# A graph-attention kernel: gathers of steps 2 and 3 held one by one, picks begun at the seventh group and three lots shorter

## The chip, the cores and the metric

The kernel runs on one core of a Trainium2 chip. The metric is the time of one execution in microseconds of the device. The kernel before has a median of 1760.69 us in 3 runs (1760.31 to 1761.43).

## What is computed

One layer of a graph network with attention over edges, followed by a residual addition and a layer norm. There are 6,250 nodes and 206,250 edges, sorted by destination, with 64 channels in 4 heads of 16.

```python
Qh = (x @ Wq.T + bq).reshape(n, H, D)
Kh = (x @ Wk.T + bk).reshape(n, H, D)
Vh = (x @ Wv.T + bv).reshape(n, H, D)
Ee = (edge_attr @ We.T + be).reshape(-1, H, D)
score = (Kh[src] * Qh[dst] * (1.0 / np.sqrt(D)) * Ee).sum(-1)
score = jnp.exp(jnp.clip(score, -5.0, 5.0))
msg = Vh[src] * score[..., None]
wV = jax.ops.segment_sum(msg, dst, num_segments=n)
x = layernorm(x + wV.reshape(n, H * D))
```

The rows of k and v at the source of every edge (`Kh[src]`, `Vh[src]`) are at random places. How they are brought to the edges is what the change is about.

## The kernel before, in words

**Tiles, groups and steps.** A tile is 128 edges, one a partition. Eight tiles are a group `g`; there are 202 groups (0 to 201, the last with four tiles). Two groups are a step, up to group 193; the last eight groups are steps of their own. A step's k and v (`kv`, 256 numbers of a row for each edge, 16 tiles) live in one of five buffers `kvs`, which are used in turn.

**The prologue.** PE multiplies all nodes by the weights (`ps`, L453), and the products go through SBUF to tables in DRAM: `kv_tab` (k and v of each node, float32) and `q3_tab`. Meanwhile POOL gathers (`collect`, L340) the x rows of the sources of the first five groups, 40 tiles, each gather being held by one of PE's matmuls. For these groups k and v are computed on the spot: ten times `x_turned` (PE, ACT), a matmul, and an addition of the bias on DVE (`first_kv`, L538), numbered i = 0 to 9. From group 5 on k and v are gathered from `kv_tab`. The gathers of groups 5, 6 and 7 (the rest of step 2, and step 3) are issued in that loop over i, behind the additions.

**Gathers.** `gather_kv` (L251) is an indirect DMA on POOL's queue: it brings 128 rows of `kv_tab`, one tile. `lots(s)` lists a step's tiles as two lots a group, and `alone` splits lots to single tiles. `gather` issues the DMAs of a lot in order, and makes the first one of the lot wait for a given instruction (`behind`), so that POOL's queue keeps a chosen place beside the other engines.

**Picks.** The last two tiles of some groups are not gathered. They are computed by PE from the node features in SBUF: for four such tiles together (a lot of picks, two groups, 512 edges) DVE makes one-hot matrices of the sources (`hots`, L640, up to five units in one instruction), and PE multiplies them with the node features, which are kept as three bf16 parts (`picks`, recorded at L680, the line of the helper `product`: 25 units of two blocks of 128 nodes, three matmuls each, 75 matmuls 128x512 a lot, accumulated in one of two PSUM banks `pick`). Then `picked` (DVE) chooses the half, `picked_kv` (PE) multiplies by the weights of k and v, and `place_kv` (ACT) puts the four tiles where the gathers would have put them. `first_unit(g)` tells at which unit iteration g starts: a lot of picks is spread over three iterations, with 9, 8 and 8 units. `when(k)` is its inverse. `LAST` is the number of lots (65). Lot m is ready in iteration `READY[m]`, and the groups it serves are `READY[m] + 4` and `READY[m] + 5`: groups (6, 7), (9, 10), (12, 13), and so on, up to (198, 199).

**The main loop.** Iteration g works on group g, and ahead of it: it issues the loads of edge features (`et`, three steps ahead), query windows (`qw`, four groups ahead) and keys (`kb`, six groups ahead) on SP's queue, and the gathers of the step four steps ahead on POOL's. On DVE: `prod` (k times the turned query-edge product `qe`), the score, one half of the hot tiles of iteration g + 1, the message `qe`, the other half, two subtractions that split the message into three bf16 parts (between them ACT makes the copies `msg`), the one-hot matrix `of` of a step (in odd iterations), the addition of a step's sums to the accumulator, and `term` for group g + 2. On PE, in this order: the edge product `ee` of group g + 3, the second half of a ready lot (`picked_kv`), the picks of iteration g, the transposes `qe` of group g + 1, the queries `qq` of group g + 2, and the sums of a step (`room`, 16 matmuls, every other iteration). On ACT: the exponential, the two halves of `to`, the two `msg` copies, `eb`.

The order of all this is written out by hand: instructions stand on each engine in the order of the source. The gathers of iteration g are held by the last matmul at several marks within the iteration (`where`). Two lines hold the picks' timetable:

```python
return UNITS * (g // 3) + (0, 9, 17)[g % 3]
LAST = max(m for m in range(1, NG) if when(UNITS * m - 1) + 5 < NG)
```

The last groups have no picks: the last lot is finished in iteration 194, and iterations 195 to 201 run without. After the last group come its sums, a layer norm of the last two blocks and their stores; the other blocks are normed and stored within the loop.

Of the kernel before, what the change touches and what calls it, by code (L numbers as in the profile page):

```python
# [22 lines left out]
NG = -(-T // G)  # L23
# [26 lines left out]
def tiles_of(g):  # L50
    return min(G, T - g * G)
# [6 lines left out]
def groups_of(s):  # L58
    return range(STEPS[s][0], STEPS[s][0] + STEPS[s][1])
# [4 lines left out]
BATCH = 4  # L64
UNITS = NB // 2
MOST = 5
XG = 5


def first_unit(g):  # L70

    return UNITS * (g // 3) + (0, 9, 17)[g % 3]


def when(k):

    return max(g for g in range(3 * k // UNITS + 3) if first_unit(g) <= k)


LAST = max(m for m in range(1, NG) if when(UNITS * m - 1) + 5 < NG)  # L80
BEGIN = [when(UNITS * m) for m in range(LAST)]
READY = [when(UNITS * m + UNITS - 1) for m in range(LAST)]
PICKED = [(READY[m] + 4, READY[m] + 5) for m in range(LAST)]
ALL_PICKED = {g for pair in PICKED for g in pair}
assert len(ALL_PICKED) == 2 * LAST and min(ALL_PICKED) > XG
assert all(BEGIN[m + 1] > BEGIN[m] + 1 for m in range(LAST - 1))

# [7 lines left out]
def is_picked(g, j):  # L95

    return g in ALL_PICKED and j >= tiles_of(g) - 2
# [23 lines left out]
def tile_gnn(ctx: ExitStack, tc: tile.TileContext, x, by_rows, xT, wT, bias, beT, weT, eT, src, src_rows, dst,  # L121
# [89 lines left out]
    def fetch_sources(m, pool):  # L211

        if m < LAST:
            SRC[m] = pool.tile([P, BATCH * P], I32, name="srcs")
            nc.sync.dma_start(SRC[m], src_rows[m:m + 1, :].to_broadcast([P, BATCH * P]))

    def sources(m, from_, odd):
        if m < LAST:
            FROM[m], ODD[m] = from_, odd
            nc.scalar.activation(FROM[m], SRC[m], AF.Identity, bias=from_row, scale=0.5)  # L220
            nc.vector.tensor_scalar(ODD[m], SRC.pop(m), 1, None, op0=OP.bitwise_and)
# [8 lines left out]
    def onehot_rows(g, to):  # L230

        n = tiles_of(g)
        TO[g] = to
        nc.scalar.activation(TO[g][:, :n, :],  # L234
                             KB.pop(g)[:, :n * P].rearrange("p (j e) -> p j e", j=n),
                             AF.Square, bias=minus_row3[:3 * W])

    def onehot_rows_rest(g):
        n = tiles_of(g)
        nc.scalar.activation(TO[g][:, :n, :], TO[g][:, :n, :], AF.Relu, bias=one_p[:3 * W],  # L240
                             scale=-1.0)

    def keys(t0):

        n = min(KEYS, T - t0)
        nc.vector.tensor_scalar(key_i[:, :n], dst_i[:, t0:t0 + n], P - 1, None, op0=OP.bitwise_and)
        nc.vector.tensor_copy(key[:, t0:t0 + n], key_i[:, :n, None].to_broadcast([P, n, 2]))
# [7 lines left out]
    def lots(s):  # L255

        some = []
        for g in groups_of(s):
            js = [j for j in range(tiles_of(g)) if not is_picked(g, j)]
            some += [(g, js[:len(js) // 2]), (g, js[len(js) // 2:])]  # L260
        return some

    def alone(some):

        return [(g, [j]) for g, js in some for j in js]
# [6 lines left out]
    def gather(lot):  # L272
        (g, js), after = lot
        for j in js:
            ins = gather_kv(g, j)
            if j == js[0]:
                behind(ins, after)

    with tc.tile_pool(name="nodes", bufs=1) as nodes, \
# [14 lines left out]
        x_nodes = slots[1][:, :30 * C], slots[3][:, :20 * C]  # L294
        src_x = nodes.tile([P, XG * G], I32, name="src_x")
        nc.scalar.dma_start(src_x, src[:, :XG * G])
        w_sb = nodes.tile([C + 1, 3 * C], F32, name="w_sb")
# [35 lines left out]
        x_rows = kvs[KVB - 1].rearrange("p t (u c) -> p (t u) c", u=2)  # L333
        XS = [x_rows[:, g * G:(g + 1) * G, :] for g in range(XG - 1)]
        XS.append(nodes.tile([P, G, C], F32, name="xs"))
        first_tiles = [(g, j) for g in range(XG) for j in range(G)]
        mark = []

        def collect(g, j):
            ins = nc.gpsimd.indirect_dma_start(  # L340
                out=XS[g][:, j, :], out_offset=None, in_=x[:, :],
                in_offset=bass.IndirectOffsetOnAxis(ap=src_x[:, g * G + j:g * G + j + 1], axis=0))
            if mark:
                behind(ins, mark[-1])
# [100 lines left out]
        for i in range(NB // CB):  # L445
            bs = slice(i * CB, (i + 1) * CB)
            kv_sb = chunks.tile([P, CB, 2 * C], F32, name="kv_sb")
            for b in range(0, CB, 2):
# [38 lines left out]
                pair = (i * CB + b) // 2  # L487
                for _ in range(1 + (pair >= NB // 2 - (XG - 1) * G + NB // 2)):
                    collect(*first_tiles.pop(0))
# [34 lines left out]
        def x_turned(g, h):  # L524
            tp = npsum.tile([P, 2, P], F32, name="tp", bufs=2)
            for u in range(2):
                j = 4 * h + 2 * u
                nc.tensor.transpose(tp[:, u, :], XS[g][:, j:j + 2, :].rearrange("p j c -> p (j c)"),
                                    ident)
            xe = nodes.tile([P, 2, P], F32, name="xe", bufs=2)  # L530
            nc.scalar.activation(xe, tp, AF.Copy)
            return xe

        def first_kv(g, h, xe):
            pv = npsum.tile([P, 4, 2 * C], F32, name="pv", bufs=2)
            for u in range(2):
                nc.tensor.matmul(pv[:, 2 * u:2 * u + 2, :], xe[:, u, :], wkv, start=True, stop=True)
            return nc.vector.tensor_add(kv_of(g)[:, 4 * h:4 * h + 4, :], pv,  # L538
                                        bkv_all[:, None, :].to_broadcast([P, 4, 2 * C]))

        def parts_of_x(i, part):

            us = slice(i * 5, (i + 1) * 5)
            xu = x_nodes[i // 3].rearrange("p (u t c) -> p u t c", t=2, c=C)[:, i % 3 * 5:][:, :5]
            if part == 2:
                nc.vector.tensor_sub(parts[:, us, 2], xu, parts[:, us, 1])
            else:
                nc.scalar.activation(parts[:, us, part], xu, AF.Copy)
                if part == 0:
                    nc.vector.tensor_sub(xu, xu, parts[:, us, 0])  # L550

        order = [(g, h) for g in range(XG) for h in range(2)]
        to_gather = lots(2)[2:] + lots(3)
        xe = x_turned(*order[0])
        for k in range(3):
            parts_of_x(k, 0)
        for i, gh in enumerate(order):
            following = x_turned(*order[i + 1]) if i + 1 < len(order) else None
            added = first_kv(*gh, xe)
            xe = following  # L560
            if i < 3:
                parts_of_x(i, 1)
                parts_of_x(i, 2)
            if i in (3, 4):
                parts_of_x(i, 0)
                parts_of_x(i, 1)
                parts_of_x(i, 2)
            if i in (1, 2, 4, 5, 6, 7):
                gather((to_gather.pop(0), added))
            if i == 5:  # L570
                sources(0, early_from, early_odd)
                keys(0)
            if i > 4 and i - 5 < 4:
                onehot_rows(i - 5, early_to[i - 5])
                onehot_rows_rest(i - 5)
# [17 lines left out]
    with tc.If(rv == 0) as branch:  # L593

        with tc.tile_pool(name="work", bufs=2) as work, \
# [32 lines left out]
            def pieces(g):  # L628

                some, k, end = [], max(first_unit(g), 0), min(first_unit(g + 1), UNITS * LAST)  # L630
                while k < end:
                    some.append((k, min(end, k + MOST, (k // UNITS + 1) * UNITS)))
                    k = some[-1][1]
                return some

            def hots(k, end):
                m, lo, hi = k // UNITS, k % UNITS, (end - 1) % UNITS + 1
                HOT[k] = work.tile([P, MOST, BATCH * P], BF16, name="hot", bufs=5)
                shape = [P, hi - lo, BATCH * P // 2, 2]
# [501 lines left out]
```

## Time and profile before

| what | value |
|---|---|
| median of 3 runs | 1760.69 us |
| the profiled execution | 1760.28 us |
| its span, first to last instruction | 1758.4 us |
| TensorE clock granted, mean | 0.990 |
| prod of group 0 starts at | 80.00 us |
| prod of group 201 starts at | 1747.27 us |
| gathers of k and v on POOL | 1312 |

A row of a timeline shows the start in us, the duration in us, the engine, the line, the operation, output and inputs, and in brackets the idle time of the engine before it, with what ended it. A row of the windows shows a stretch, its length, the busy time and number of instructions of PE, PEld (PE's weight loads), DVE, ACT and POOL, the granted clock, the share of the DMA engines' time and GB/s. A row of the groups shows line, engine, operation, names and count, then the busy time in us, the mean of one in ns, the idle time of the engine before them, and what ended most of it. In the chain rows stand the start, the duration and what the chain ran through.

### The profile page before, as it was taken

To read this page: it belongs to the slowest core of one execution; us is meant where nothing else is said; L and a number is where in the kernel's file an instruction comes from. 1 tells how busy PE (TensorE), PEld (TensorE's weight loads), DVE (VectorE), ACT (ScalarE), POOL (GpSimd) and SP (SyncE) were. 2 spreads that over 40 slices of the span, in tenths; PEclk is the share of its full clock that TensorE was granted. 3 is DMA by queue.
4 is the path that set the end of the run, shared out by engine and by line. 5 is a ranking of instruction groups with operands and counts; after the bars stand their busy time and mean duration, and the time that the engine had idled before them with its cause. 6 is when DMAs were issued, how large, how long until landed. Compare 5 with 4: busy or idle time off the path is not lost.

```text
span 1758.4 us, 27231 instructions
## 1 busy us (share of the span) xinstructions
PE 1697.8 (97%) x8717; PEld 900.2 (51%) x8863; DVE 1599.2 (91%) x2711; ACT 924.7 (53%) x1516; POOL 1303.4 (74%) x1362
## 2 busy tenths in 40 slices
PE   6799999999999999999999999999999999999994
PEld 6445555555555555455555555555555555555543
DVE  5699999999999999999999999999999999999987
ACT  3655555555555555555555545545555555555553
POOL 6777777777777777777777777777777777777752
PEclk9999999999999999999999999999999999999996
DMA  6844444434444445444444444444544434445431
GB/s 190 273 131 120 140 120 127 138 110 139 139 113 140 124 122 141 119 140 129 124 139 116 131 139 111 136 138 118 144 119 135 138 110 138 138 116 144 120 95 29
DMA packets 141939, 229.89 MB, mean 131 GB/s; under 512 B 70369, under 2 KB 71115, under 8 KB 141673
## 3 DMA queue, kind: packets, MB, share of 16 engines
q1 hardware_dynamic: 98086, 139.63, 26.6%
q0 software_dynamic: 43264, 87.38, 19.2%
q8 instruction: 71, 1.16, 0.3%
q10 hardware_dynamic: 436, 1.04, 0.3%
q14 instruction: 82, 0.67, 0.1%
HBM read 220.11 MB, written 7.81 MB: 130 GB/s over the span
## 4 chain that ended last, share of the span: by engine, by line
PE 77%; DVE 12%; DMA 5%; ACT 2%; issue 2%; POOL 1%; SPq 0%; DVEq 0%; ACTq 0%; POOLq 0%
PE pick L680 54%; PE ee L680 10%; PE room L680 6%; PE qe L709 4%; DMA kv<-kv_tab,src_i 4%; DVE hot L640 3%; PE qq L680 3%; DVE score L731 1%; DVE prod L728 1%; DVE term L704 1%; PE ps L453 1%; DVE qe L749 1%; ACT msg L761 1%; DVE qe L766 1%; POOL kv L251 1%
## 5 line engine op out<-in xcount | busy, mean ns | idle before, releaser
L251 POOL DMA_INDIRECT kv<-kv_tab,src_i x1312 | 1263.6, 963 | 411.2 <-issue 162.2
L680 PE MATMUL pick<-hot,parts 128*128 128x512 bf16 x4729 | 1073.7, 379 | 7.7
L680 PEld LDWEIGHTS <-parts 128*128 128x128 bf16 x4875 | 477.2, 98 | 604.6 <-issue 74.7
L640 DVE TENSOR_TENSOR hot<-from,still 128x2560 bf16<-128x2560 bf16 (+2 forms) x384 | 482.4, 1256 | 0.0
L737 ACT ACTIVATE score<-score 128x32 f32<-128x32 f32 x202 | 46.3, 229 | 624.8 <-DVE score L733 620.5
L761 ACT ACTIVATE msg<-qe 128x512 bf16<-128x512 f32 x400 | 238.8, 597 | 154.0 <-DVE qe L749 132.7
L680 PE MATMUL ee<-et,we_sb 128*128 128x512 f32 x404 | 223.4, 635 | 5.5 <-ACT eb L691 4.1
L240 ACT ACTIVATE to<-to,one_p 126x1024 bf16<-126x1024 bf16 x198 | 226.4, 1144 | 0.0
L234 ACT ACTIVATE to<-kb,minus_row 126x1024 bf16<-126x1024 bf16 x198 | 223.8, 1130 | 0.0
L766 DVE TENSOR_TENSOR msg<-qe,msg 128x512 bf16<-128x512 f32 x200 | 136.9, 685 | 70.8 <-ACT msg L761 70.7
L680 PE MATMUL room<-msg,of 128*128 128x192 bf16 x1592 | 150.9, 248 | 16.8 <-DVE acc L803 16.8
L704 DVE TENSOR_TENSOR term<-eb,qq 128x512 f32<-128x512 f32 x202 | 136.7, 677 | 20.6 <-PE qq L680 15.7
L680 PEld LDWEIGHTS <-of 128*128 128x128 bf16 x1600 | 128.9, 99 | 40.5 <-issue 36.6
L731 DVE TENSOR_REDUCE score<-prod 128x32 f32<-128x512 f32 x202 | 138.3, 685 | 7.0
L766 DVE TENSOR_TENSOR qe<-qe,msg 128x512 f32<-128x512 f32 x200 | 138.0, 690 | 4.8 <-ACT msg L761 4.8
L691 ACT ACTIVATE eb<-ee,be_col 128x512 f32<-128x512 f32 x202 | 139.7, 692 | 4.7 <-PE ee L680 4.7
L728 DVE TENSOR_TENSOR prod<-kv,qe 128x512 f32<-128x512 f32 x202 | 137.2, 679 | 5.0 <-issue 2.1
L749 DVE TENSOR_TENSOR qe<-kv,score 128x512 f32<-128x512 f32 x200 | 138.9, 695 | 1.8 <-ACT score L737 1.8
L709 PE MATMUL qe<-ident,term 128*128 128x128 f32 x806 | 122.7, 275 | 1.0 <-DVE term L704 0.9
L720 DVE TENSOR_TENSOR of<-still,key 128x2048 bf16<-128x2048 bf16 (+2 forms) x105 | 122.6, 1168 | 0.2
L709 PEld LDWEIGHTS qe<-ident,term 128*128 128x128 f32 x806 | 101.5, 142 | 41.7 <-DVE term L704 1.9
L680 PE MATMUL qq<-to,qw 126*64 126x512 bf16 x396 | 80.7, 404 | 0.0
(136 smaller groups left out, 875.1 us busy)
## 6 DMA issues: line engine op xcount, KB each, us to landing
et<-in_eT SPq DMA_DIRECT2D x100, 512.0 KB
kb<-key_tab SPq DMA_DIRECT2D x201, 252.0 KB
kv<-kv_tab,src_i POOLq DMA_INDIRECT x1312
srcs<-in_src_rows SPq DMA_DIRECT2D x65, 256.0 KB
qw<-q_tab SPq DMA_DIRECT2D x202, 15.8 KB
kv_tab<-kv_sb SPq DMA_DIRECT2D x4, 640.0 KB
q_tab<-q SPq DMA_DIRECT2D x5, 480.0 KB
acc<-in_x SPq DMA_DIRECT2D x48, 32.0 KB
```

The lines of the kernel that those rows point to most:

```text
L234: nc.scalar.activation(TO[g][:, :n, :], KB.pop(g)[:, :n * P].rearrange("p (j e) -> p j e", j=n), AF.Square, bias=minus_row3[:3 * W])
L240: nc.scalar.activation(TO[g][:, :n, :], TO[g][:, :n, :], AF.Relu, bias=one_p[:3 * W], scale=-1.0)
L251: return nc.gpsimd.indirect_dma_start(out=kv_of(g)[:, j, :], out_offset=None, in_=kv_tab[:, :], in_offset=bass.IndirectOffsetOnAxis(ap=src ...
L640: nc.vector.tensor_tensor(HOT[k][:, :hi - lo].rearrange("p b (a c) -> p b a c", c=2), pairs(FROM[m])[:, None].to_broadcast(shape), block2[ ...
L680: mark.append(nc.tensor.matmul(*aps, **kw))
L704: nc.vector.tensor_mul(TERM[g][:, :n], EB.pop(g)[:, :n], qq[:, :n])
L709: nc.tensor.transpose(qe[g % 2][:, 2 * u:2 * u + 2, :].rearrange("p j c -> p (j c)"), TERM[g][:, u, :], ident)
L728: nc.vector.tensor_mul(prod[:, :n, :], kv_of(g)[:, :n, :C], qe[g % 2][:, :n, :])
L731: nc.vector.tensor_reduce(score, prod[:, :n, :].rearrange("p g (h d) -> p g h d", h=H), axis=AX.X, op=OP.add)
L749: nc.vector.tensor_mul(to.rearrange("p g (h d) -> p g h d", h=H), kv_of(g)[:, :n, C:].rearrange("p g (h d) -> p g h d", h=H), SCORE[g][:, ...
L761: nc.scalar.activation(part, left, AF.Copy)
L766: nc.vector.tensor_sub(left if i == 0 else part_of(g, 2)[1], left, part)
```

## The change

Three things are changed, and all else stays.

- The picks begin in iteration 6 (`LEAD`) and not in iteration 0. Lot m keeps its three iterations and its distance to the groups it serves, so the first lot now serves groups 12 and 13. Groups 6, 7, 9 and 10 are gathered whole.
- `LAST` is computed with 8 in place of 5. There are 62 lots, the last of which is finished in iteration 191 and serves groups 195 and 196. Groups 198 and 199 are gathered whole. With the four tiles of each lot that is gone, 1,324 tiles are gathered in place of 1,312.
- In the prologue the gathers of groups 5, 6 and 7 are 24 in place of 20. They are single tiles (`alone`), each held by the addition of k and v after which it is issued: two after each of the additions 0 to 4, three after each of 5 to 8, two after 9. Before, lots of four and three were issued after the additions 1, 2, 4, 5, 6 and 7, and only the first of a lot was held.

```diff
+LEAD = 6
 XG = 5
 def first_unit(g):
-    return UNITS * (g // 3) + (0, 9, 17)[g % 3]
+    return UNITS * ((g - LEAD) // 3) + (0, 9, 17)[(g - LEAD) % 3]
 def when(k):
-    return max(g for g in range(3 * k // UNITS + 3) if first_unit(g) <= k)
+    return max(g for g in range(LEAD + 3 * k // UNITS + 3) if first_unit(g) <= k)
-LAST = max(m for m in range(1, NG) if when(UNITS * m - 1) + 5 < NG)
+LAST = max(m for m in range(1, NG) if when(UNITS * m - 1) + 8 < NG)
...
-        to_gather = lots(2)[2:] + lots(3)
+        to_gather = alone(lots(2)[2:] + lots(3))
...
-            if i in (1, 2, 4, 5, 6, 7):
+            for _ in range(3 if 4 < i < 9 else 2):
                 gather((to_gather.pop(0), added))
```

Lines after the new one stand one lower in the changed kernel: L251 becomes L252.

## The prediction

> **What bounds the kernel now.** First the page: how full each engine is, and the chain that ended last.
>
> ```profile
> span 1758.4 us, 27231 instructions
> PE 1697.8 (97%) x8717; PEld 900.2 (51%) x8863; DVE 1599.2 (91%) x2711; ACT 924.7 (53%) x1516; POOL 1303.4 (74%) x1362
> PE 77%; DVE 12%; DMA 5%; ACT 2%; issue 2%; POOL 1%; SPq 0%; DVEq 0%; ACTq 0%; POOLq 0%
> ```
>
> PE looks like the bound and POOL like an idle engine. The groups and a window of six iterations in mid-run (the last row counts POOL's gathers up to 1679.7 us) say more:
>
> ```profile
> L251 POOL DMA_INDIRECT kv<-kv_tab,src_i x1312 | 1263.6, 963 | 411.2 <-issue 162.2
> L728 DVE TENSOR_TENSOR prod<-kv,qe 128x512 f32<-128x512 f32 x202 | 137.2, 679 | 5.0 <-issue 2.1
> ...
> 329.90:380.00 50.10, 49.89 (x263) 25.91 (x265) 46.60 (x77) 26.18 (x42) 38.00 (x40) 1.00 0.45 125
> ...
> L251 POOL DMA_INDIRECT kv<-kv_tab,src_i x1280 | 1233.2, 963 | 390.5 <-issue 156.7 <-PE pick L680 95.4 <-DMA kv<-kv_tab,src_i 60.4
> ```
>
> In 50.10 us PE is busy 49.89 at clock 1.00: the loop runs at PE's pace, 8.35 us an iteration. But POOL is just as full in another sense. Its 1,280 gathers up to 1679.7 us take 963 ns plus 390.5/1280 = 305 ns of "idle" each, and 0.30 us is the gap that stands before a gather even when nothing is waited for (rows below). So POOL issues without a pause, one gather in (1233.2 + 390.5)/1280 = 1.268 us. The prod row says that this hurts nobody: in 202 iterations the first reader of the gathered rows was kept idle 5.0 us. What remains is how far POOL is ahead:
>
> ```profile
> 56.21 0.95 POOL L251 DMA_INDIRECT kv<-kv_tab,src_i  x1 [0.30 <-DVE parts L546]
> ...
> 1569.69 0.94 POOL L251 DMA_INDIRECT kv<-kv_tab,src_i  x1 [0.30 <-PE pick L680]
> ...
> 1678.50 1.07 POOL L251 DMA_INDIRECT kv<-kv_tab,src_i  x1 [0.30 <-PE pick L680]
> 1682.54 0.94 POOL L251 DMA_INDIRECT kv<-kv_tab,src_i  x1 [2.96 <-PE qq L680]
> 1699.87 0.94 POOL L251 DMA_INDIRECT kv<-kv_tab,src_i  x1 [7.65 <-PE qq L680]
> 1708.30 0.94 POOL L251 DMA_INDIRECT kv<-kv_tab,src_i  x1 [1.25 <-PE room L680]
> 1729.71 0.94 POOL L251 DMA_INDIRECT kv<-kv_tab,src_i  x1 [0.30 <-PE room L680]
> ```
>
> Counting gathers by group, 1569.69 is the last of group 183 and 1678.50 that of group 196. Only for groups 197, 198 and 199 is POOL held by PE (2.96, 7.65 and 1.25 us, less 0.30 each: 10.96 in all). The last gather starts at 1729.71, 28.7 us before the end.
>
> **The change part by part.** *Counts.* Sixty-five lots of picks (25 units of three matmuls) become 62, and iterations 0 to 5 and 192 to 201 have none; before, only 195 to 201. Gone are 225 pick matmuls on PE, 18 hot tiles on DVE, three srcs loads on SP's queue. Added are 12 gathers on POOL: four in groups 6 and 7, four in 9 and 10, four in 198 and 199. Inside 6 to 191 every lot keeps its place by threes and by even and odd groups, so the loop keeps its pace.
>
> *The stretch that goes.* DVE's timeline gives the iterations by their prod (iterations 177, 186, 194, 195 and 201 here):
>
> ```profile
> 1555.93 0.68 DVE L728 TENSOR_TENSOR prod<-kv,qe 128x512 f32<-128x512 f32 x1
> ...
> 1634.70 0.69 DVE L728 TENSOR_TENSOR prod<-kv,qe 128x512 f32<-128x512 f32 x1
> ...
> 1701.09 0.69 DVE L728 TENSOR_TENSOR prod<-kv,qe 128x512 f32<-128x512 f32 x1 [0.19 <-issue]
> 1704.53 0.70 DVE L766 TENSOR_TENSOR qe<-qe,msg 128x512 f32<-128x512 f32 x1 [0.82 <-ACT msg L761]
> 1706.06 0.69 DVE L766 TENSOR_TENSOR msg<-qe,msg 128x512 bf16<-128x512 f32 x1 [0.23 <-ACT msg L761]
> 1707.26 0.68 DVE L728 TENSOR_TENSOR prod<-kv,qe 128x512 f32<-128x512 f32 x1
> ...
> 1747.27 0.41 DVE L728 TENSOR_TENSOR prod<-kv,qe 128x256 f32<-128x256 f32 x1
> ```
>
> The new kernel has 186 iterations with picks, like iterations 0 to 185 of the old one; the other nine, 1707.26 - 1634.70 = 72.56 us, go, and nine without picks come. Such an iteration is shown by 1701.09 to 1707.26: 6.17 us, not PE's but the chain prod, score, exp, msg on ACT, subtraction, msg, term, in which DVE waits for ACT.
>
> *The front* (DVE's timeline again).
>
> ```profile
> 76.86 0.69 DVE L704 TENSOR_TENSOR term<-eb,qq 128x512 f32<-128x512 f32 x1 [1.68 <-ACT eb L691]
> 77.47 2.61 DVE L640 TENSOR_TENSOR hot<-y,still 128x2560 bf16<-128x2560 bf16 x2
> 80.00 0.68 DVE L728 TENSOR_TENSOR prod<-kv,qe 128x512 f32<-128x512 f32 x1
> ...
> 92.15 1.21 DVE L720 TENSOR_TENSOR of<-still,key 128x2048 bf16<-128x2048 bf16 x1
> ...
> 109.53 0.35 DVE L797 TENSOR_REDUCE room<-room 128x64 f32<-128x192 f32 x1
> ...
> 110.11 0.68 DVE L704 TENSOR_TENSOR term<-eb,qq 128x512 f32<-128x512 f32 x1
> ...
> 118.68 0.68 DVE L728 TENSOR_TENSOR prod<-kv,qe 128x512 f32<-128x512 f32 x1
> ...
> 127.04 0.68 DVE L728 TENSOR_TENSOR prod<-kv,qe 128x512 f32<-128x512 f32 x1
> ```
>
> The two hot tiles at 77.47 go, so prod 0 starts 2.53 us sooner. Iterations 0, 2 and 4 take 6.17. Odd ones also make `of` (about 1.14 to the next start), of which 0.92 hides in the wait for ACT (1704.53 + 0.61 to 1706.06): 6.39, and with the add of iteration 3 (109.53 to 110.11, 0.58) 6.97. Iteration 5 already makes the hot tiles of iteration 6 and takes what it takes now, 127.04 - 118.68 = 8.36. Sum: 3 x 6.17 + 6.39 + 6.97 + 8.36 = 40.23, less 2.53: 37.70. From there PE must do at once what it had not to do in old iteration 0, the sums of a step (the chain in order of time):
>
> ```profile
> 80.18 5.56 PE pick L680 x25
> ...
> 100.70 1.43 PE room L680 x16
> ```
>
> so +1.43. (The pick row prices what left: 225 x 5.56/25 = 50 us of PE, only partly replaced by shorter work, since the nine iterations are now DVE's and ACT's.)
>
> *PE's clock.* An idle PE is a new state for the front. The windows of the tail show one (the third number from the end is the clock).
>
> ```profile
> 1720.00:1740.00 20.00, 10.10 (x43) 6.10 (x40) 16.97 (x40) 8.63 (x16) 8.21 (x9) 0.69 0.17 43
> 1740.00:1760.00 20.00, 8.81 (x42) 7.72 (x42) 10.76 (x35) 5.01 (x9) 0.00 (x0) 0.50 0.03 8
> ```
>
> With PE half busy the granted clock fell to 0.69 and 0.50, so the first picks of iteration 6 may run at half speed. Bounds: nothing (the window at 329.90, clock 1.00) to a whole iteration's 5.56 us of picks done twice as slowly; I take 1.7, nearer the lower end, because work comes back without a gap. The Trainium skill, "TensorE: Matmul & The Clock Gate", Part 1, speaks against the change here: the array falls to half its clock after an idle window of some 3.4 us and needs as long a busy one to come back. By that rule an estimate of the loss is half of 3.4, about 1.7 us; the falling clock in the two rows agrees with it.
>
> *The tail.* Iterations 192, 193 and 194 cost 6.17, 6.39 + 0.78 for a full add, 6.17: 19.5. Their x pick and copies replace the same in 195 and 196. Loop alone: 1758.4 - 72.56 + 37.70 + 1.43 + 1.7 + 19.5 = 1746.2.
>
> *The gathers.* Eight more by group 196 and no pause: the gather at 1678.50 moves to 1688.6 (8 x 1.268). Its holds vanish, because PE's marks come 12 us sooner and POOL 10 us later. From there 36 gathers instead of 32, at 1.249 (the spacing in the last rows, 0.94 + 0.30) to 1.268: the last starts at 1733.6 to 1734.3. Landing:
>
> ```profile
> 1704.86 2.38 DMA kv<-kv_tab,src_i
> ```
>
> 2.38 us from start: 1736.0 to 1736.7, where prod 201 can begin; now it is followed by 1758.4 - 1747.27 = 11.1 us. End by the gathers: 1747.1 to 1747.8. The loop alone would bring prod 201 at 1735.1, so **POOL sets the end, at 1747.5**. Waiting for k and v one by one costs nothing: POOL reaches the prologue's gathers after 40 others, when the addition named is done. The bound above is that each of the 24 shows its wait as the row below does, 0.41 - 0.30 = 0.11, 2.6 us in all; I take nothing, since the gathers that were held before (56.21) have a gap of 0.30. A gain is excluded: no gather goes away.
>
> ```profile
> 18.10 0.94 POOL L340 DMA_INDIRECT kv<-in_x,src_x  x1 [0.41 <-PE ps L453]
> ```
>
> In mid-run POOL's lead shrinks. Group 183 is the tightest: its last gather, 1569.69 + 10.1 + 2.4 = 1582.2, against its prod, now where iteration 177 was plus 37.7 + 1.43 + 1.7: 1596.8. Some 14 us are left.
>
> The profiled execution took 1760.28 us, 1.88 over its span; the median of the runs is 0.41 above it. 1747.5 + 1.88 + 0.41 = 1749.8; I say **1749.5 us**, 0.6% faster.
>
> **The rivals.** *The front does not run faster* (DMA busy share there is high, and edges, keys and q windows could land late): six iterations at 8.36 are 50.2 instead of 40.2, the end 1756.2 and the time 1758.5, no change. For it: DMA is at its fullest between 60 and 80 us. Against it: prods 0 to 3 follow now without idle time on DVE. *POOL paces the whole loop.* If the loop follows the gathers at a fixed distance, the 28.7 us after the last gather stay, and 12 gathers x 1.268 = 15.2 us come on top, less at most the 10.96 of holds: the end at 1762.6 to 1773.6, 1765 to 1776 us. For it: POOL never rests, and the chain has DMA links. Against it: the 5.0 us of idle before prod. It decides once the 14 us of lead are used up. *Holds stay, gathers no brake*: if gathers land in time, the loop's own 1746.2 stands: 1748.5.
>
> **How the numbers follow.** About 0.2%, 3.5 us, is what a measurement can tell from no change. Forecast, with the last rival, which is its lower edge: 0.76. Front not faster: 0.12, of which a third still counts as faster. POOL paces: 0.12. So faster 0.80, same 0.08, slower 0.12. The range begins at 1745.5 (loop alone, no clock loss, and a us for the norm batches that shift) and ends at 1758.5, the first rival's time.
>
> **What would show it.** Right: prod 0 near 77.5, prod 6 near 118, pick matmuls from there; a granted clock under 1.00 between 80 and 120 us; POOL without a hold after 56 us, its last gather near 1734; DVE idle before the last prods, released by kv's DMA. Wrong: iterations 0 to 4 at 7 us or more; POOL holds in the tail; DVE idle before prod in mid-run (then POOL paces); iterations 6 to 191 not at 8.35 us, the one premise under all the sums.

## The result, and the profile after

The changed kernel took 1749.67 us, the median of 6 runs (1748.15 to 1750.26), and the kernel before beside it 1762.55 us (6 runs, 1760.31 to 1765.35). The ratio is 0.9924, with a 95% interval of 0.9912 to 0.9937: 0.76% faster. The profiled execution took 1748.15 us, its span is 1746.4 us. The loop's own end in the prediction was 1746.2. (Three of the chips used for the experiments ran the kernel before itself at 2,050 to 2,078 us; each ratio below is against the kernel before on the same chip.)

The page of the changed kernel, with its first rows and the groups of the gathers and of prod (line, engine, operation, count, busy us, mean ns, idle us before them):

```profile
span 1746.4 us, 26827 instructions
PE 1673.3 (96%) x8611; PEld 884.7 (51%) x8611; DVE 1577.0 (90%) x2687; ACT 919.5 (53%) x1507; POOL 1309.7 (75%) x1374
...
L252 POOL DMA_INDIRECT kv<-kv_tab,src_i x1324 | 1269.8, 959 | 403.5 <-issue 171.0
L729 DVE TENSOR_TENSOR prod<-kv,qe 128x512 f32<-128x512 f32 x202 | 137.4, 680 | 5.1 <-issue 1.7
```

The 12 more gathers are there, and prod still waits only 5.1 us in 202 iterations. (A gathered row is 128 numbers of float32, 64 of k and 64 of v; where the kernel is described above, 256 is a slip on which no step rests.) A gather now takes 959 ns and 403.5/1324 = 305 ns before it, 1.264 us in all; in the kernel before it was 963 + 313, of which 11 us in all were holds. Four nanoseconds look like nothing, but times 1,324 they are 5.3 us, and that is the point on which the predicted end turned.

DVE's timeline of the changed kernel (start, duration, engine, line, operation, and in brackets the idle time before). The prods are those of groups 0, 5, 6, 7, 192, 193, 194, 195 and 201:

```profile
78.71 0.68 DVE L729 TENSOR_TENSOR prod<-kv,qe 128x512 f32<-128x512 f32 x1
...
110.51 0.68 DVE L729 TENSOR_TENSOR prod<-kv,qe 128x512 f32<-128x512 f32 x1
...
118.88 0.68 DVE L729 TENSOR_TENSOR prod<-kv,qe 128x512 f32<-128x512 f32 x1
...
127.69 0.68 DVE L729 TENSOR_TENSOR prod<-kv,qe 128x512 f32<-128x512 f32 x1
...
193.11 0.68 DVE L729 TENSOR_TENSOR prod<-kv,qe 128x512 f32<-128x512 f32 x1
...
1674.83 0.68 DVE L729 TENSOR_TENSOR prod<-kv,qe 128x512 f32<-128x512 f32 x1
...
1680.98 0.68 DVE L729 TENSOR_TENSOR prod<-kv,qe 128x512 f32<-128x512 f32 x1
...
1688.47 0.36 DVE L816 COPY y<-acc 128x64 f32<-128x64 f32 x1
...
1689.50 0.69 DVE L729 TENSOR_TENSOR prod<-kv,qe 128x512 f32<-128x512 f32 x1 [0.19 <-issue]
...
1695.85 0.68 DVE L729 TENSOR_TENSOR prod<-kv,qe 128x512 f32<-128x512 f32 x1
...
1735.45 0.41 DVE L729 TENSOR_TENSOR prod<-kv,qe 128x256 f32<-128x256 f32 x1
```

(193.11 is group 15.) These rows split the span as the prediction split it:

| stretch | predicted | measured | difference |
|---|---|---|---|
| up to prod 0 | 77.47 | 78.71 | +1.24 |
| iterations 0 to 5 | 40.23 | 118.88 - 78.71 = 40.17 | -0.06 |
| iterations 6 to 191 | 1554.70 + 1.43 + 1.7 = 1557.83 | 1674.83 - 118.88 = 1555.95 | -1.88 |
| iterations 192 to 194 | 19.5 | 1695.85 - 1674.83 = 21.02 | +1.5 |
| prod 195 to the end | 1758.4 - 1707.26 = 51.14 | 1746.4 - 1695.85 = 50.55 | -0.59 |
| the loop alone | 1746.2 | 1746.4 | +0.2 |

POOL's timeline in the changed kernel, with its first and its last gather of k and v:

```profile
55.90 0.94 POOL L252 DMA_INDIRECT kv<-kv_tab,src_i  x1 [0.30 <-DVE parts L547]
...
1727.81 1.17 POOL L252 DMA_INDIRECT kv<-kv_tab,src_i  x1 [0.30 <-issue]
```

The last gather starts at 1727.81 and not at 1733.6 to 1734.3. Prod 201 has no bracket at 1735.45: it did not wait. So in this execution the loop set the end, not POOL. It is the shortest of the six, 1.5 us under their median, and the others left no trace. The kernel with a busy PE (below) has the same gathers and a traced execution at its median, and there too prod 201 did not wait.

The windows of the changed kernel (stretch, length, busy time of PE, PEld, DVE, ACT, POOL, granted clock, DMA share, GB/s):

```profile
60.00:80.00 20.00, 15.88 (x36) 7.70 (x36) 7.86 (x14) 13.27 (x17) 15.42 (x16) 0.57 0.93 291
80.00:100.00 20.00, 12.11 (x48) 6.21 (x48) 14.47 (x25) 12.51 (x20) 15.12 (x17) 0.83 0.59 181
100.00:120.00 20.00, 10.44 (x37) 5.40 (x38) 17.00 (x29) 10.82 (x17) 15.12 (x17) 0.70 0.37 106
...
121.60:140.00 18.40, 18.40 (x96) 9.21 (x95) 15.83 (x28) 8.74 (x14) 13.93 (x15) 1.00 0.46 128
1680.00:1700.00 20.00, 13.27 (x49) 7.70 (x50) 15.73 (x30) 10.99 (x19) 15.12 (x17) 0.74 0.41 111
```

With PE busy 12.11 and 10.44 us of 20 the granted clock is 0.83 and 0.70; it is 1.00 in the stretch from 121.60 on, 2.6 us after the first pick starts at 118.99 (its row stands further down). POOL's busy time is the same 15.12 in the front, and in the tail too, where it used to be held.

### The profile page after: what moved, and what is told of

Same layout as the page of the kernel before. It is cut to its first block, busy times and chain, and to the rows that moved or that the text cites. A ratio compares the mean times of both kernels' runs of the same rounds, so it can differ in the third digit from the quotient of the medians.

```text
span 1746.4 us, 26827 instructions
## 1 busy us (share of the span) xinstructions
PE 1673.3 (96%) x8611; PEld 884.7 (51%) x8611; DVE 1577.0 (90%) x2687; ACT 919.5 (53%) x1507; POOL 1309.7 (75%) x1374
## 4 chain that ended last, share of the span: by engine, by line
PE 74%; DVE 12%; DMA 7%; ACT 3%; issue 2%; POOL 1%; DVEq 0%; SPq 0%; ACTq 0%; POOLq 0%
PE pick L681 51%; PE ee L681 9%; DMA kv<-kv_tab,src_i 6%; PE room L681 6%; PE qe L710 4%; DVE hot L641 3%; PE qq L681 3%; DVE score L732 1%; DVE prod L729 1%; DVE term L705 1%; POOL kv L252 1%; PE ps L454 1%; DVE qe L750 1%; ACT msg L762 1%; DVE qe L767 1%
## 5 line engine op out<-in xcount | busy, mean ns | idle before, releaser
L252 POOL DMA_INDIRECT kv<-kv_tab,src_i x1324 | 1269.8, 959 | 403.5 <-issue 171.0
L681 PE MATMUL pick<-hot,parts 128*128 128x512 bf16 x4650 | 1035.3, 380 | 0.0
L681 PEld LDWEIGHTS <-parts 128*128 128x128 bf16 x4650 | 455.0, 98 | 578.8 <-issue 73.6
L641 DVE TENSOR_TENSOR hot<-from,still 128x2560 bf16<-128x2560 bf16 x366 | 460.4, 1258 | 0.0
L681 PE MATMUL ee<-et,we_sb 128*128 128x512 f32 x404 | 229.3, 650 | 30.1 <-ACT eb L692 28.7
L681 PE MATMUL room<-msg,of 128*128 128x192 bf16 x1592 | 153.4, 251 | 16.1 <-DVE acc L804 16.1
L681 PEld LDWEIGHTS ee<-et,we_sb 128*128 128x128 f32 x404 | 62.2, 194 | 59.2 <-ACT eb L692 40.0
```

The source lines that it names most:

```text
L252: return nc.gpsimd.indirect_dma_start(out=kv_of(g)[:, j, :], out_offset=None, in_=kv_tab[:, :], in_offset=bass.IndirectOffsetOnAxis(ap=src ...
L641: nc.vector.tensor_tensor(HOT[k][:, :hi - lo].rearrange("p b (a c) -> p b a c", c=2), pairs(FROM[m])[:, None].to_broadcast(shape), block2[ ...
L681: mark.append(nc.tensor.matmul(*aps, **kw))
```

## The experiments

The three runs on a chip where the kernel before took 1,763 us decide, and come first. The nine on the slower chips, whose engines pause for a reason that the profile doesn't show, follow.

### Picks from the thirteenth group on

The number of first iterations without picks is doubled:

```diff
-LEAD = 6
+LEAD = 12
```

This gives 60 lots and 1,332 gathers. It tells POOL as a brake at the end from POOL as the loop's pace and from a loop that doesn't see POOL.

> Picks from iteration 12 once more (60 lots, 1,332 gathers), to meet the undisturbed condition of the first measurement, in which before took 1760 to 1765 us. There: loop theory without any brake 1738.7; with the gathers as a brake at the end 1753 to 1755; POOL paces at a fixed distance 1760. With the pauses present again (before over 2,000 us): the ratio 1.0072 (1.0045 to 1.0099) again.

Measured: 1756.02 us (1755.05 to 1758.34) against 1762.74, ratio 0.9962 (0.9948 to 0.9977). So it is 6 us slower than the changed kernel, although six more iterations lack their picks. DVE's prods of the last four groups in its timeline, and POOL's last gather and the groups of the gathers and of prod behind them:

```profile
1719.50 0.69 DVE L729 TENSOR_TENSOR prod<-kv,qe 128x512 f32<-128x512 f32 x1 [2.98 <-DMA kv<-kv_tab,src_i]
...
1729.75 0.69 DVE L729 TENSOR_TENSOR prod<-kv,qe 128x512 f32<-128x512 f32 x1 [3.04 <-DMA kv<-kv_tab,src_i]
...
1740.01 0.69 DVE L729 TENSOR_TENSOR prod<-kv,qe 128x512 f32<-128x512 f32 x1 [3.92 <-DMA kv<-kv_tab,src_i]
...
1745.64 0.42 DVE L729 TENSOR_TENSOR prod<-kv,qe 128x256 f32<-128x256 f32 x1 [1.90 <-DMA kv<-kv_tab,src_i]
```

```profile
1742.23 1.21 POOL L252 DMA_INDIRECT kv<-kv_tab,src_i  x1 [0.30 <-issue]
```

```profile
L252 POOL DMA_INDIRECT kv<-kv_tab,src_i x1332 | 1281.5, 962 | 406.4 <-issue 188.8
...
L729 DVE TENSOR_TENSOR prod<-kv,qe 128x512 f32<-128x512 f32 x202 | 137.7, 682 | 23.4 <-DMA kv<-kv_tab,src_i 16.1
```

Here each of the last prods is released by its gathers, and the prods follow at some 10.2 us (1719.50 to 1729.75), which is eight gathers at 1.25 and a little. Prod 201 starts 3.4 us after the last gather does (1742.23 to 1745.64), then come 1756.6 - 1745.64 = 11.0 us. This is the end that the prediction had seen for the changed kernel. Of the three theories the brake at the end holds. A loop without a brake would have been much faster than the changed kernel; a loop at POOL's pace throughout would have shown such brackets all along, and there are 16.1 us of them in 11 iterations, most of it in the last six groups. At prod 192 this kernel was still 5.2 us ahead of the changed one (1669.65 for 1674.83), at prod 201 it was 10.2 us behind (1745.64 for 1735.45). A miss in size: the last gather came at 1742.23, 4 us later than expected. A gather took (1281.5 + 406.4)/1332 = 1.267 us and not the 1.264 of the changed kernel's execution.

### The front alone

The three lots at the end are put back; picks still begin in iteration 6 (1,320 gathers):

```diff
-LAST = max(m for m in range(1, NG) if when(UNITS * m - 1) + 8 < NG)
+LAST = max(m for m in range(1, NG) if when(UNITS * m - 1) + 5 < NG)
```

> Picks from iteration 6, but up to iteration 194 (63 lots, 1,320 gathers), once more beside the kernel before, for the undisturbed condition. Loop theory: the changed kernel less its tail, 2.7 us slower than the changed kernel (prod 192 to prod 195 takes 23.75 us in place of 21.02), a ratio of 0.994 against before, and POOL held again between groups 196 and 200. POOL theory (the last gather sets the end in the changed kernel): four gathers fewer, 5 us faster than the changed kernel, 0.990.

Measured: 1753.52 us (1750.6 to 1754.81) against 1762.64, ratio 0.9946 (0.9932 to 0.9960). DVE's timeline with prods 192, 195 and 201, and POOL's last gather:

```profile
1676.80 0.68 DVE L729 TENSOR_TENSOR prod<-kv,qe 128x512 f32<-128x512 f32 x1
...
1700.53 0.68 DVE L729 TENSOR_TENSOR prod<-kv,qe 128x512 f32<-128x512 f32 x1
...
1740.65 0.41 DVE L729 TENSOR_TENSOR prod<-kv,qe 128x256 f32<-128x256 f32 x1
```

```profile
1726.10 0.96 POOL L252 DMA_INDIRECT kv<-kv_tab,src_i  x1 [0.30 <-issue]
```

Iterations 192 to 194 take 1700.53 - 1676.80 = 23.73 us here and 21.02 in the changed kernel: leaving their picks out is worth 2.7 us there, and the iterations around them gain as well: from prod 186 to prod 201 it is 1740.65 - 1627.97 = 112.68 us here and 1735.45 - 1626.62 = 108.83 in the changed kernel, 3.85 us. The ratio is the loop's 0.994, not 0.990, which would follow if the end went with POOL's last gather. That gather comes 14.5 us ahead of prod 201. So the front brings about 9 us of the 12.9 and the tail the rest. The holds of POOL in groups 197 to 199, which I expected back, didn't come: POOL's last gathers all stand 0.30 or 0.31 behind the one before. I take it, without a run for it, that the eight more gathers in groups 6, 7, 9 and 10 (8 x 1.25 = 10 us) and PE's marks, which come some 7 us sooner (prod 197 at 1716.66 for 1723.32), had used up the 10.96 us of holds.

### PE kept busy in iterations 0 to 5

Sixteen matmuls whose result nobody reads are added in each of the first iterations:

```diff
+            def warm(g):
+                if g < LEAD:
+                    for u in range(8):
+                        nc.tensor.matmul(px[1][:, :6 * C], parts[:, u, 0].rearrange("p t c -> p (t c)"),
+                                         parts[:, u].rearrange("p i t c -> p (i t c)"),
+                                         start=True, stop=True)
...
+                warm(g)
...
+                warm(g)
```

> The changed kernel with 16 unused matmuls in each of the iterations 0 to 5, once more for the undisturbed condition. Clock theory: granted clock near 1.00 between 80 and 120 us (0.83 and 0.70 in the changed kernel), prod 6 to prod 7 down from 8.82 us by 1.7 at most, and the time by 1 to 2 us, a ratio of 0.991 to 0.992 against before. Rival: iteration 6 stays at 8.8 us, or the added matmuls make the front longer than the 40.17 us it takes from prod 0 to prod 6.

Measured: 1748.32 us (1746.12 to 1751.35) against 1762.64, ratio 0.9921 (0.9907 to 0.9935): no difference from the changed kernel that the intervals would show. Its windows, then PE's timeline around the first picks, then prods 6, 7 and 201 on DVE and POOL's last gather:

```profile
80.00:100.00 20.00, 17.92 (x104) 10.26 (x104) 14.46 (x25) 12.48 (x21) 14.44 (x17) 1.00 0.61 178
100.00:120.00 20.00, 14.58 (x80) 7.86 (x80) 17.00 (x29) 10.99 (x17) 15.42 (x16) 0.96 0.41 107
...
119.10:122.00 2.90, 2.90 (x8) 1.08 (x8) 2.83 (x6) 1.27 (x2) 2.24 (x3) 0.56 0.80 247
122.00:126.00 4.00, 4.00 (x22) 1.95 (x20) 3.14 (x6) 3.25 (x5) 3.08 (x4) 1.00 0.59 175
```

```profile
113.20 1.47 PE L686 MATMUL pick<-parts 128*128 128x384 bf16 x8
117.28 1.17 PE L681 MATMUL ee<-et,we_sb 128*128 128x512 f32 x2 [2.61 <-ACT eb L699]
...
119.10 6.83 PE L681 MATMUL pick<-hot,parts 128*128 128x512 bf16 x25 [0.22 <-issue]
```

```profile
119.04 0.68 DVE L736 TENSOR_TENSOR prod<-kv,qe 128x512 f32<-128x512 f32 x1
...
127.35 0.68 DVE L736 TENSOR_TENSOR prod<-kv,qe 128x512 f32<-128x512 f32 x1
...
1735.10 0.41 DVE L736 TENSOR_TENSOR prod<-kv,qe 128x256 f32<-128x256 f32 x1
```

```profile
1728.93 0.95 POOL L252 DMA_INDIRECT kv<-kv_tab,src_i  x1 [0.30 <-issue]
```

The clock of the front rose from 0.83 and 0.70 to 1.00 and 0.96, and iterations 0 to 5 stayed as long (78.86 to 119.04, 40.18). So their 6.2 us is not a matter of PE's clock. That DVE and ACT set it, as predicted, is read from DVE's waits for ACT's `msg`, 0.82 us twice in iteration 4 of the changed kernel; no run shortened the work of either. But the filler ends at 114.67, PE then waits 2.61 us, and the clock is down to 0.56 just when the picks begin. The 25 picks took 6.83 us, 0.273 each. In PE's timeline of the changed kernel the same place reads:

```profile
117.12 2.07 PE L681 MATMUL ee<-et,we_sb 128*128 128x512 f32 x2 [5.32 <-ACT eb L692]
118.99 7.28 PE L681 MATMUL pick<-hot,parts 128*128 128x512 bf16 x27
```

There the gap was 5.32 us, and a pick took 7.28/27 = 0.270 us. Iteration 6 came down from 8.81 us to 127.35 - 119.04 = 8.31, and not by the 1.7 hoped for; in the run with the front alone, whose front is that of the changed kernel, it took 9.40, so 0.5 us is no more than such iterations differ without a filler. The run therefore tells that the filler costs nothing and that no gain of it shows. It doesn't measure the clock loss itself, because the filler left the gap that matters. At the end of this execution, which took the median time, the last gather starts 1735.10 - 1728.93 = 6.2 us ahead of prod 201, which did not wait.

### One part alone, and other lengths, on chips with pauses

Four kernels on one chip, 5 rounds each, where the kernel before took 2077.81 us.

The front alone, the same edit as above:

> The changed kernel with 63 lots: picks from iteration 6, but up to iteration 194 as before, so only groups 6, 7, 9 and 10 are gathered in addition (1,320 gathers). Loop theory (nine iterations without picks pay, POOL has room at the end): the tail's part is lost, which the two traces give as 23.75 us (prod 192 to prod 195 before) less 21.02 us (after), so some 2.7 us slower than the changed kernel, about 1752.4. POOL theory (the last gather sets the end): four gathers fewer, 5 us faster, about 1744.6.

Measured 2079.62, ratio 1.0009 (0.9994 to 1.0023).

The tail alone, in the kernel before:

```diff
-LAST = max(m for m in range(1, NG) if when(UNITS * m - 1) + 5 < NG)
+LAST = max(m for m in range(1, NG) if when(UNITS * m - 1) + 8 < NG)
```

> The kernel before, with 64 lots: picks from iteration 0, none in iterations 192 to 194 (1,316 gathers). Loop theory: 2.7 us faster than before, about 0.15%. POOL theory: four gathers more in groups 198 and 199, 5.1 us slower than before, or no change if the 10.96 us for which POOL was held there take them up.

Measured 2070.59, ratio 0.9978 (0.9965 to 0.9990).

The holds one by one alone, in the kernel before:

```diff
-        to_gather = lots(2)[2:] + lots(3)
+        to_gather = alone(lots(2)[2:] + lots(3))
-            if i in (1, 2, 4, 5, 6, 7):
+            for _ in range(2):
```

> The kernel before with the prologue's 20 gathers one by one, two behind each of the ten additions; picks as before. Loop theory: no change, POOL reaches these gathers when the additions are done. If each wait costs 0.11 us of POOL's time, the 20 cost 2.2 us of POOL's lead and still nothing of the end. Rival (holds delay the gathers): POOL's 21st gather of k and v would start later than 81.84 us by over 2 us.

Measured 2076.53, ratio 0.9995 (0.9985 to 1.0005).

The changed kernel with the old holds:

```diff
-        to_gather = alone(lots(2)[2:] + lots(3))
+        to_gather = lots(2)[2:] + lots(3)
-            for _ in range(3 if 4 < i < 9 else 2):
+            if i in (1, 2, 4, 5, 6, 7):
```

> The changed kernel with the prologue's 24 gathers in six lots of four behind the additions 1, 2, 4, 5, 6 and 7, only the first of a lot held, as before. Loop theory: the same as the changed kernel within 1 us, 1749.7. Rival (the new holds are what brings part of the gain, or cost up to 2.6 us): 2 us or more off.

Measured 2079.04, ratio 1.0004 (0.9987 to 1.0020). The expectations were made for 1,760 us and miss where the front is concerned. DVE's prods 0 and 6 of the kernel with the old holds and picks from iteration 6, then those of the one with the new holds and picks from iteration 0:

```profile
102.32 0.68 DVE L729 TENSOR_TENSOR prod<-kv,qe 128x512 f32<-128x512 f32 x1
...
162.03 0.68 DVE L729 TENSOR_TENSOR prod<-kv,qe 128x512 f32<-128x512 f32 x1
```

```profile
101.13 0.68 DVE L728 TENSOR_TENSOR prod<-kv,qe 128x512 f32<-128x512 f32 x1
...
156.66 0.68 DVE L728 TENSOR_TENSOR prod<-kv,qe 128x512 f32<-128x512 f32 x1
```

Six iterations without picks take 59.7 us there, and six with picks 55.5: with such pauses the front isn't shorter, and the change loses its largest part. The tail still pays (0.9978 for it alone). The holds make no difference that shows: 0.9995 put in, and with the old ones the changed kernel is at 1.0004 where the changed kernel itself stood at 0.9989 on another chip with pauses.

Four more on another such chip (5 rounds, the kernel before 2049.9 us): nine and twelve iterations without picks (`LEAD = 9`, `LEAD = 12`), the filler of above, and `+ 11` in place of `+ 8` in `LAST` (61 lots, the tail three iterations longer).

> The changed kernel with picks from iteration 9: 61 lots, 1,328 gathers. Loop theory without any brake: three iterations of 25.05 us with picks become 19.5 us without, 5.5 us faster than the changed kernel, about 1744. Loop with the gathers as a brake at the end: the last gather starts 4 x 1.264 us later, at 1732.9, lands 2.38 us later and is followed by 11 us, so a span of 1746.3 and about 1748.2 to 1749.5, hardly any gain. POOL paces at a fixed distance: 5 us slower, about 1755.

> The changed kernel with picks from iteration 12: 60 lots, 1,332 gathers. Loop theory without any brake: 11 us faster than the changed kernel, about 1738.7. With the gathers as a brake at the end: last gather at 1737.9, span 1751.3, 1753 to 1755, slower than the changed kernel by 4 to 5 us. POOL paces at a fixed distance: 10 us slower, about 1760.

> The changed kernel with 16 matmuls 128x384 bf16 more in each of the iterations 0 to 5 on PE, which compute nothing that is used; they keep PE busy there. Clock theory: the granted clock stays nearer 1.00 between 80 and 120 us, the iteration of the first picks (prod 6 to prod 7), 8.82 us in the changed kernel, comes down by about 1.7 us, and the time by as much, to about 1748. Rival (what slows iteration 6 is the sums and the late term, not the clock): no change of iteration 6, or a slower front because of the added matmuls.

> The changed kernel with one more lot dropped at the tail: 61 lots, 1,328 gathers, the last picks in iteration 188. Loop theory without any brake: 3.2 us faster than the changed kernel (24.2 us become 21.0), about 1746.5. With the gathers as a brake: last gather at 1732.9, about 1748.2 to 1749.5. POOL paces at a fixed distance: 5 us slower, about 1755.

Measured: `LEAD = 9` 2059.69, ratio 1.0038 (1.0019 to 1.0057); `LEAD = 12` 2065.48, 1.0072 (1.0045 to 1.0099); the filler 2052.11, 1.0005 (0.9989 to 1.0021); the longer tail 2049.07, 0.9985 (0.9967 to 1.0003). From the filler's kernel (six iterations without picks) to nine and to twelve, each three more cost there 0.33 to 0.34%. Nothing of these ratios can be carried to the undisturbed chip. Nine iterations and the longer tail weren't run there, so whether one of them beats the changed kernel is open.

Last, the changed kernel itself on a third chip with pauses, where the kernel before took 2077.93 us:

> The changed kernel itself, timed once more beside the kernel before, because in the runs of the parts every kernel, the one before included, took 2,040 to 2,080 us, with pauses on all engines that end on nothing the profile shows. Loop theory: where those pauses are absent, 0.9924 of before again (0.9912 to 0.9937). Where they are present, the front's six iterations without picks need their instructions sooner than they come and take as long as iterations with picks; the gain is gone, and the ratio is 1.000 within 0.002. Rival (the changed kernel gains by its shorter PE work whatever the pauses): 0.992 to 0.995 also there.

Measured: 2076.93, ratio 0.9989 (0.9977 to 1.0001). As expected for a chip with pauses, the gain is gone. Two rows of its timelines around 135 us, on ACT and PE, and its group of weight loads for the sums, then the same group in the kernel before on the undisturbed chip:

```profile
134.60 0.69 ACT L692 ACTIVATE eb<-ee,be_col 128x512 f32<-128x512 f32 x1 [10.88 <-remote]
```

```profile
135.34 2.07 PE L681 MATMUL ee<-et,we_sb 128*128 128x512 f32 x2 [15.25 <-ACT eb L692]
```

```profile
L681 PEld LDWEIGHTS <-of 128*128 128x128 bf16 x1600 | 133.3, 101 | 154.8 <-issue 149.9
```

```profile
L680 PEld LDWEIGHTS <-of 128*128 128x128 bf16 x1600 | 128.9, 99 | 40.5 <-issue 36.6
```

ACT stood still for 10.88 us, and nothing that the profile records ended it ("remote" is what the profile says of a releaser that it doesn't know). The instructions are as long as elsewhere, 101 ns a load against 99; what grows is time in which an engine waits for nothing visible, 149.9 us against 36.6 before the same 1,600 loads. What stops the engines is open; that instructions come too late, as the expectation has it, no run shows. That the front is no shorter under such pauses is seen; which of the pauses fall there because of the change was not told apart.

## Why the prediction was right, and where it was off

The time was predicted as 1749.5 us and came out at 1749.67. That the two agree to 0.2 us is in part luck. The end that the trace shows is the loop's, for which the prediction's own sum gave 1748.5; the loop's five stretches missed by up to 1.9 us each (table above) and cancelled to 0.2; and the median lay 1.5 us above the profiled execution where the prediction had added 0.4. Point by point:

**The stretch that goes and the loop's pace** were right. Iterations 15 to 191 took 1674.83 - 193.11 = 1481.72 us. They were to be iterations 9 to 185 of the kernel before, which took 1634.70 - 152.37 = 1482.33 (the row of 152.37 stands further down).

**The front** was right: 40.17 for 40.23 us, and the run with a busy PE shows that PE's clock has no part in it. The rival by which it doesn't run faster fell on the undisturbed chip. Its outcome is what came on the chips with pauses; its reason, loads that land late, was not shown there.

**Prod 0** was 1.24 us late, in work that the change doesn't touch. The same four matmuls of the prologue, in PE's timeline before and after:

```profile
61.47 1.13 PE L537 MATMUL pv<-wkv,xe 128*128 128x256 f32 x4 [1.61 <-ACT xe L531]
```

```profile
61.27 2.07 PE L538 MATMUL pv<-wkv,xe 128*128 128x256 f32 x4 [1.61 <-ACT xe L532]
```

After the same gap of 1.61 us they ran at full speed once and at about half speed the other time. The Trainium skill, "TensorE: Matmul & The Clock Gate", Part 1, says that the activity window runs freely and that the point of the switch shifts with where the first matmul falls in it; these two rows agree. From 60 to 80 us the granted clock was 0.57 in the changed kernel (row above) and 0.91 in the kernel before. The change is not needed for it: the kernel before with only its tail changed has the same prologue, and in PE's timeline of that run, on a chip with pauses, the four matmuls are slow too (what sets the moment of the switch was not varied):

```profile
70.20 2.08 PE L537 MATMUL pv<-wkv,xe 128*128 128x256 f32 x4 [1.61 <-ACT xe L531]
```

**The sums of a step and the clock** were priced at 1.43 + 1.7 = 3.13 us on top of the old iterations. DVE's timeline of the kernel before has prods 1 and 9 at

```profile
87.16 0.68 DVE L728 TENSOR_TENSOR prod<-kv,qe 128x512 f32<-128x512 f32 x1
...
152.37 0.68 DVE L728 TENSOR_TENSOR prod<-kv,qe 128x512 f32<-128x512 f32 x1
```

so its first nine iterations took 152.37 - 80.00 = 72.37 us, and the first nine with picks now took 193.11 - 118.88 = 74.23: 1.86 more, 1.27 less than priced. The first has 1.65 of it (8.81 from 118.88 to 127.69, for 87.16 - 80.00 = 7.16), the other eight together 0.21. (Among these single iterations differ by up to 1.8 us either way, because a block of nodes closes in iteration 7 of both kernels.) The first picks of the kernel before, in PE's timeline:

```profile
79.75 5.99 PE L680 MATMUL pick<-hot,parts 128*128 128x512 bf16 x26
```

They took 5.99 us and began 0.25 us before prod 0. In the changed kernel they took 7.28 and began 0.11 after prod 6, behind an `ee` of 2.07 us where the kernel before has 1.12. That is 1.29 + 0.36 = 1.65, and as prod 7 follows a `term` that waits for PE's `qq` behind these picks, it makes up the whole of the first iteration. So what that iteration lost, it lost to PE's half speed (granted clock 0.50 from 117.12 to 121.60): 1.65 us for the 1.7 priced. The sums stand on PE behind that `qq` (126.98 for 126.64), where they don't lengthen this iteration; of their 1.43 no more than the 0.21 shows in the other eight, and 0.20 and 0.21 in the runs with a busy PE and with the front alone. Theirs is the term of the two that was too large.

**The tail** was 1.5 us too short in the sum: iteration 193 took 1689.50 - 1680.98 = 8.52 us for the 7.17 expected. A block of nodes closed there, and its copy and statistics (1688.47 to 1689.50 in DVE's rows) are 1.0 us that I had not counted to it. Against the front alone it paid 2.7 us in iterations 192 to 194 and 3.85 from prod 186 on.

**The gathers: the step that failed.** "POOL sets the end, at 1747.5" rested on 1.268 us for each of 1,324 gathers, and the last one was to start at 1733.6 to 1734.3. It started at 1727.81, because a gather took 1.264 us in this execution. The term was mis-sized by 4 ns a gather. So the two signs named for POOL's end, a last gather near 1734 and DVE idle before the last prods, did not come. The mechanism exists, as the run with twelve iterations without picks shows, but it did not act here. The landing was sized too small as well: 2.38 us were taken from the last gather's start to prod 201, and that run has 3.4. With 3.4 us from the last gather's start to prod 201, measured there, the changed kernel had 1735.45 - 1727.81 - 3.4 = 4.2 us to spare, or 3 ns a gather. At 1.268 the last would have started at 55.9 + 1323 x 1.268 = 1733.5 (55.9 is where POOL's first one starts) and held prod 201 by some 1.4 us. What was listed as a rival, the loop's own end of 1746.2, is what came, though without the holds that the rival named. The number held because the two ends were only 1.3 us apart.

**The holds** went as predicted: none after 56 us, with 403.5/1324 = 0.305 us before a gather, the plain gap. That single holds in the prologue cost nothing agrees with this and with 0.9995 for them alone, though that was measured only on a chip with pauses. **POOL as the pace of the whole loop** fell: prod's idle time stayed at 5.1 us, and doubling the iterations without picks made waits for gathers almost only in its last groups.

## What to carry to other kernels

A queue that never rests needs its own line in the sum: count its pieces, multiply, and compare its last landing with the moment at which the loop wants it; with 1,324 pieces a few nanoseconds each decide which of the two is late. Taking work off the engine that bounds pays only down to the next chain, here 6.2 us an iteration over DVE and ACT, and only until the queue behind takes over: six iterations without picks gained, twelve gave 6 us back. Before trusting a ratio, look at what the kernel before takes on the same chip.

## What the runs showed that was not expected

The mean length of a gather differs between executions, 959 to 963 ns in the undisturbed runs, with the same 0.30 us ahead of it; most take 0.94 or 0.95, and 79 to 97 in an execution take over 1.0, up to 1.47. It isn't the kernel alone: the one with a busy PE has 959 ns on the undisturbed chip and 966 on a chip with pauses. After a gap of only 2.61 us on PE, behind a stretch with a mean clock of 0.96, the granted clock fell to 0.56 for some 3 us and was 1.00 from 122.00 on. And three chips ran this one-core kernel at 2,050 to 2,078 us, 16 to 18% over the 1,762 of the others, with the same lengths of prod and of the gathers (681 and 961 ns in the changed kernel there) and with pauses of 10 us and more on nothing visible (10.88 in the row above); on the one where the changed kernel itself was timed, the change of 0.76% shrank to 0.11%, with an interval that takes in no change.
